# A new stored order of stretches and a new row of PSUM pairs in a hand-ordered Nystrom attention and expert FFN kernel

## The chip, the cores and the metric

The kernel runs on one core of a Trainium2 chip. The metric is device time in microseconds, the median over several runs of the same compiled program. Everything is one launch.

## The reference, cut to what matters

The input `x` has 16 batches of 1024 rows of 256 values, all float32. Each batch passes through a Nystrom attention and then through an FFN with a choice of one expert of eight.

```python
x = x + layernorm(attention(layernorm(x)))
x = x + layernorm(ffn(layernorm(x)))

# attention: 16 heads of 16 values, 64 landmarks
Q, K, V = split(x @ w_qkv); Q = Q / 4
Q_l, K_l = means of Q and K over groups of 16 rows
kernel1 = softmax(Q @ K_l.T); kernel2 = softmax(Q_l @ K_l.T); kernel3 = softmax(Q_l @ K.T)
SV = (kernel1 @ inverse(kernel2)) @ (kernel3 @ V)     # inverse by 6 iterations of 64x64 products
out = SV @ w_proj

# ffn
recon_e = relu(x @ Wd1[e] + bd1[e]) @ Wd2[e] + bd2[e]     # for all 8 experts
idx = the expert with the least mean of (recon_e - x)**2, for each batch
out = x @ W_base + b_base + relu(x @ Wa_down[idx] + ba_down[idx]) @ Wa_up[idx] + ba_up[idx]
```

## The kernel before, in words

Every batch passes through five pieces of work, each written as a Python generator that yields at the start of each **stretch**, a handful of instructions that belong together.

- `stage_a(b)` makes Q, K and V of batch b and the part `kernel3 @ V`. Its stretches: `stats` and `xn` (normalisation, on DVE), `qk` (matmuls `pq`, L475), `v` (`pv`, L500), `max` (`psm`, L547, with a DVE reduction `mx`, L556), `mcol` and `mrow` (row maxima), `e3` (scores `psc`, L567 and L578, and ACT's exponential, L588), `ut` (`put`, L604, with a DVE addition, L614) and `u` (a transpose `pu`, L653).
- `stage_p(b)` makes the inverse of kernel2. Its stretches are a serial chain: `k2`, `k2n`, `sums`, `kv0`, then six times `l` (matmuls `pxl`, then ACT's copy `qw`, L780), `h` (DVE, L783) and `q` (matmuls `pxq`, then DVE's L787 and L762), and `end`.
- `stage_c(b)` makes kernel1, the product and the projection. Its stretches: `max` (`psc`, L823, with the DVE reduction `most`, L831, and then POOL's `maxima`, L340 to L344), `mt` (a transpose `pm`, L853), `e1` (`psct`, L862 and L870, with ACT's exponential, L880), `sv` (`psv`, L891), `po` (`po`, L926, with ACT's copies and squares, L420 and L423, and POOL's `rstd`, L371) and `out` (DVE, L411).
- `stage_d1(b)` makes the experts' losses. Its stretches: `stats`, `xn`, `xt` (transposes `pt_d`, L404), `ht` (`ph`, L999), `df` (`pr`, L1029, with DVE's subtraction, L1037, and ACT's two squares, L1040), `pe` (a DVE reduction, L1057), `gather` (a matmul `pl`, L1062, and DVE's choice of the expert, then two DMA loads from SP) and `wup`.
- `stage_d2(b)` makes the FFN's output. Its stretches: `a` (`pad`, L1125, with ACT's `a_t`, L1134), `po` (`pf`, L1145 to L1158) and `out` (DVE, L411, and the store from SP).

Five streams run through these stages: stage a over all batches, stage p, stage c, the FFN of all batches but number 14, and the FFN of batch 14 alone. A stored string, `ORDER`, has one digit for each stretch: the stream that takes the next step. No planner runs when the kernel is built. The loop that emits the instructions does only this:

```python
    with tc.manual_schedule(engines={mybir.EngineType.PE, mybir.EngineType.Activation, mybir.EngineType.DVE, mybir.EngineType.Pool}):
        for k in order:
            next(emitted[k], None)
```

So the instructions of PE, ACT, DVE and POOL stand, on each engine, in the order of the digits, and each engine works through its own list in that order. Semaphores hold an instruction back until its data or its buffer is there. An order can therefore not make the result wrong, but it decides who waits.

The second string, `PAIRS`, decides buffers. All matmul results go to PSUM, whose eight banks are used as four pairs. Each request for a result tile takes the pair that the next digit names, and its first matmul waits until whoever held that pair before has been read out:

```python
    pairs = iter(PAIRS)

    def two_banks(shape, name, dtype=F32):
        return ps2 if isinstance(ps2, Nothing) else ps2.tile(shape, dtype, tag=f"ps2_{next(pairs)}", name=name)
```

Three buffers in SBUF matter below. The tile of `kt` is used again for the normalised rows `xn` of the next batch, so `xn` waits for the last `e3` of this batch. `x1` has two buffers, so `max` of stage c for batch b follows the FFN's end of batch b-2. And the last batch lends some buffers of earlier stages. In `turned_rows` and `stage_d2` the last batch also runs 20 and 16 matmuls without use (`spare`, L157) ahead of its transposes and of `pad`.

## Time and profile before

| what | value |
|---|---|
| median of 3 runs | 1941.46 us (1941.35 to 1944.79) |
| profiled execution, its own time | 1940.27 us |
| its span, first to last instruction | 1938.1 us |
| instructions in the span | 81528 |
| PE busy | 1844.0 us, 95% of the span |
| weight loads (PEld) busy | 1265.7 us, 65% |
| DVE busy | 1511.4 us, 78% |
| ACT busy | 1133.1 us, 58% |
| POOL busy | 212.1 us, 11% |
| granted TensorE clock, mean | 0.990 |

The profiled execution took 2.2 us more than its span, and 1.2 us less than the median. In the views, a line gives a start and a duration in us, the engine, the source line, the operation, the tiles as out<-in, the shape and a count; the bracket at the end is the idle time of the engine just ahead, and who ended it. "issue" there means that nothing that the profile shows was being waited for.

### The profile page before, as it was taken

To read this page: it belongs to the slowest core of one execution; us is meant where nothing else is said; L and a number is where in the kernel's file an instruction comes from. 1 tells how busy PE (TensorE), PEld (TensorE's weight loads), DVE (VectorE), ACT (ScalarE), POOL (GpSimd) and SP (SyncE) were. 2 spreads that over 40 slices of the span, in tenths; PEclk is the share of its full clock that TensorE was granted. 3 is DMA by queue.
4 is the path that set the end of the run, shared out by engine and by line. 5 is a ranking of instruction groups with operands and counts; after the bars stand their busy time and mean duration, and the time that the engine had idled before them with its cause. 6 is when DMAs were issued, how large, how long until landed. Compare 5 with 4: busy or idle time off the path is not lost.

```text
span 1938.1 us, 81528 instructions
## 1 busy us (share of the span) xinstructions
PE 1844.0 (95%) x37175; PEld 1265.7 (65%) x37175; DVE 1511.4 (78%) x2805; ACT 1133.1 (58%) x2434; POOL 212.1 (11%) x423
## 2 busy tenths in 40 slices
PE   6789999999999999999999999999999999989898
PEld 5667578567585766677676666866758485755544
DVE  6787878878788787787788887888788877686664
ACT  1243745573847557665655756557474667456576
POOL 1001001001110101101010010101101010010101
PEclk9899999999999999999999999999999999999899
DMA  8011011102020110111110111110201110010101
GB/s 203 3 25 25 3 28 47 24 18 56 7 67 3 51 24 12 40 29 46 28 34 15 29 45 28 46 24 8 67 7 46 24 51 2 7 46 7 45 6 48
DMA packets 65767, 64.30 MB, mean 33 GB/s; under 512 B 9244, under 2 KB 65424, under 8 KB 65424
## 3 DMA queue, kind: packets, MB, share of 16 engines
q1 hardware_dynamic: 65424, 59.11, 11.7%
q8 instruction: 291, 4.77, 1.0%
q14 instruction: 52, 0.43, 0.1%
HBM read 42.32 MB, written 16.78 MB: 30 GB/s over the span
## 4 chain that ended last, share of the span: by engine, by line
PE 78%; DVE 11%; ACT 5%; issue 2%; DMA 2%; POOL 1%; SPq 1%; DVEq 0%; POOLq 0%; ACTq 0%
PE ph L999 10%; PE pq L475 10%; PE pr L1029 10%; PE pf L1158 6%; PE pv L500 5%; PE po L926 5%; PE psv L891 4%; PE psct L862 3%; PE psc L823 3%; PE psm L547 3%; PE pxl L698 3%; PE psc L578 3%; PE pxq L698 3%; PE put L604 2%; DVE mx L556 2%
## 5 line engine op out<-in xcount | busy, mean ns | idle before, releaser
L1040 ACT ACTIVATE df<-df,bd_sb 128x512 f32<-128x512 f32 x512 | 362.7, 711 | 80.8 <-DVE df L1037 80.6
L1037 DVE TENSOR_TENSOR df<-pr,xt_d 128x1024 f32<-128x1024 f32 x256 | 298.7, 1215 | 58.2 <-PE pr L1029 45.6
L475 PE MATMUL pq<-xa,wqkv_sb 32*128 32x256 f32 x4096 | 242.5, 382 | 15.6 <-DVE xa L390 15.4
L1029 PE MATMUL pr<-ht,wd_sb 64*64 64x512 f32 x2048 | 245.6, 599 | 1.0 <-ACT ht L1007 0.2
L999 PE MATMUL ph<-xt_d,wd_sb 128*128 128x512 f32 x512 | 236.5, 604 | 2.1 <-issue 0.9
L475 PEld LDWEIGHTS pq<-xa,wqkv_sb 32*128 32x128 f32 x4096 | 219.4, 187 | 28.9 <-DVE xa L390 15.4
L556 DVE TENSOR_REDUCE mx<-psm 128x2 f32<-128x1024 f32 x128 | 149.8, 1217 | 37.4 <-PE psm L547 36.9
L999 PEld LDWEIGHTS ph<-xt_d,wd_sb 128*128 128x128 f32 x512 | 92.0, 189 | 116.2 <-issue 94.4
L831 DVE TENSOR_REDUCE most<-psc 128x16 f32<-128x1024 f32 x128 | 150.2, 1216 | 14.1 <-PE psc L823 13.9
L880 ACT ACTIVATE e<-psct 128x1024 f32<-128x1024 f32 x128 | 123.8, 1019 | 60.9 <-PE psct L870 60.6
L1029 PEld LDWEIGHTS pr<-ht,wd_sb 64*64 64x64 f32 x2048 | 67.6, 132 | 120.5 <-issue 56.4
L588 ACT ACTIVATE e<-psc 128x1024 f32<-128x1024 f32 x128 | 122.9, 1025 | 31.4 <-PE psc L578 30.9
L926 PE MATMUL po<-wproj_sb,svn 32*128 32x256 f32 x2048 | 126.9, 380 | 1.5 <-DVE svn L962 1.4
L1007 ACT ACTIVATE ht<-ph,bd_sb 128x1024 f32<-128x1024 f32 x64 | 70.9, 1108 | 93.7 <-PE ph L999 93.5
L500 PE MATMUL pv<-wqkv_sb,xa 32*128 32x256 f32 x2048 | 124.7, 379 | 0.1
L926 PEld LDWEIGHTS po<-wproj_sb,svn 32*128 32x128 f32 x2048 | 108.7, 185 | 19.4 <-DVE df L1037 4.9
L1158 PE MATMUL pf<-wbase_sb,xt_d 128*128 128x256 f32 x512 | 120.0, 388 | 0.0
L500 PEld LDWEIGHTS pv<-wqkv_sb,xa 32*128 32x128 f32 x2048 | 109.3, 185 | 6.9 <-issue 1.0
L1158 PEld LDWEIGHTS pf<-wbase_sb,xt_d 128*128 128x128 f32 x512 | 95.3, 191 | 22.7 <-issue 10.9
L783 DVE SCALAR_TENSOR_TENSOR q<-qw,eye 128x512 f32<-128x512 f32 x96 | 65.2, 679 | 45.1 <-ACT qw L780 44.7
L787 DVE SCALAR_TENSOR_TENSOR xw<-xw,pxq 128x640 f32<-128x640 f32 x96 | 69.7, 726 | 39.2 <-PE pxq L698 38.4
L1040 ACT ACTIVATION_READ_ACCUMULATOR df<-df,bd_sb 128x1 f32 x512 | 96.7, 189 | 0.0
(185 smaller groups left out, 3054.7 us busy)
## 6 DMA issues: line engine op xcount, KB each, us to landing
x<-in_L_attn_x_dram SPq DMA_DIRECT2D x16, 1024.0 KB
xa<-in_L_attn_x_dram SPq DMA_DIRECT2D x60, 256.0 KB
out_dram<-y_d SPq DMA_DIRECT2D x30, 512.0 KB
wqkv_sb<-in_L_attn_w_qkv_dram SPq DMA_DIRECT2D x12, 256.0 KB
wup<-in_L_ffn_Wa_up_dram SPq DMA_DIRECT2D x30, 64.0 KB
xa<-in_L_attn_x_dram SPq DMA_DIRECT2D x8, 128.0 KB
wproj_sb<-in_L_attn_w_proj_dram SPq DMA_DIRECT2D x4, 256.0 KB
out_dram<-y_d SPq DMA_DIRECT2D x4, 256.0 KB
```

Source lines behind the costliest of these rows:

```text
L475: nc.tensor.matmul(pq[g // 2][:, g % 2, 0 : N // 4], lhsT=wqkv_sb[rows32(g), k, f0 : f0 + P], rhs=turned[rows32(g), k], start=(k == 0), st ...
L500: nc.tensor.matmul(pv[g // 2][:, g % 2, 0:D], lhsT=turned[rows32(g), k, t0 // 4, :], rhs=wqkv_sb[rows32(g), k, 2 * D : 3 * D], start=(k == 0),
L556: nc.vector.tensor_reduce(mx3[:, n, q : q + 2], psc[g], X, ALU.max)
L588: nc.scalar.activation(e, psc[g], AF.Exp)
L831: nc.vector.tensor_reduce(mx[:, t0 : t0 + 2, 2 * g : 2 * g + 2].rearrange("x t p j -> x p t j"), psc[g].rearrange("x p t c (r l) -> x p t ...
L880: nc.scalar.activation(e, psc[g], AF.Exp)
L926: nc.tensor.matmul(po[g // 2][:, g % 2, 0:D], lhsT=svt[rows32(g), k, :], rhs=wproj_sb[rows32(g), k, :], start=(k == 0), stop=(k == ND - 1),)
L999: nc.tensor.matmul(ph[:, n, :], lhsT=wd1_sb[:, k, 2 * i : 2 * i + 2, :].rearrange("p e h -> p (e h)"), rhs=xt[:, k, n * 512 : (n + 1) * 51 ...
L1029: nc.tensor.matmul(pr[to, r, :], lhsT=wd2_sb[half, i, k * P + 64 * f : k * P + 64 * f + 64], rhs=ht[half, cols], start=True, stop=True,)
L1037: nc.vector.tensor_tensor(df, pr, middle(xt[:, k, cols], 2), ALU.subtract)
L1040: nc.scalar.activation(df[:, r, :], df[:, r, :], AF.Square, bias=bd2_sb[:, e, k : k + 1], accum_out=part[:, e, k * NW + n : k * NW + n + 1],)
L1158: nc.tensor.matmul(banks[j // 2][:, j % 2, :], lhsT=xt[:, k, cols], rhs=wbase_sb[:, k, :], start=False, stop=(j % 2 == 1 and k == NC - 1),)
```

## The change

Both stored strings are replaced: `ORDER` (1648 digits, the same number of each digit) and `PAIRS` (1634 digits). Nothing else in the file differs. Each engine gets the same instructions with the same shapes, in another sequence; result tiles land in other PSUM pairs; and the number of stand-alone semaphore instructions, which are put in where an instruction has more than one wait, goes from 335 to 325 on PE, from 416 to 403 on DVE and from 302 to 286 on ACT.

```diff
 ORDER = (
-    "0000020000012000000000000011000000012110130011010010110121010110120101201100000122120122020000202012"
-    "0112120112312013021310332001312132013303102333301301000133100030113003000330101102121023130112012213"
+    "0000020000010100000000001000000000111210130010100112012012101011001021100010010122120122020000202012"
+    "2131021011212003103301033001301333010100033313320120102001203333310001011102311013221021331102001221"
...
-    "3231333131231133331323331321133133122313122311312113121133212331224424422442224224422244444224244442"
-    "344423333334333443333343343333333433443333244333"
+    "2012212232113133313313312213331321233121232131131233133213312222244441421242244224224422424444224244442434"
...
 PAIRS = (
-    "0123012301230123012301230123012301203120312032103120312031203120310321032013201320123102310321032103"
+    "0123012301230123012301230123013201230123012301230123012301230123012031023103210321302123012013201320"
...
```

Written out as stretches (stream letter, batch, name), four places that the prediction speaks of. A stretch that only touches DVE or ACT is listed where it is emitted.

The start, after `p.0.k2`:

```
before: c.0.max.0.0 a.0.v.1 a.0.max.0.0 a.0.max.1.0 a.0.max.0.1 a.0.max.1.1 a.0.mcol a.0.mrow a.0.e3.0 ... a.0.u p.0.kv0 c.0.max.0.2 p.0.l0 p.0.h0 a.1.qk.0.0 p.0.q0
after:  a.0.v.1 p.0.k2n a.0.max.0.0 a.0.max.1.0 a.0.max.0.1 a.0.max.1.1 a.0.mcol a.0.mrow a.0.e3.0 ... a.0.u p.0.kv0 p.0.l0 p.0.h0 c.0.max.0.0 p.0.q0 a.1.qk.0.0
```

The choice of the expert of batch 13:

```
before: d.13.df.3.1.0 d.13.df.3.1.1 p.15.l2 c.14.e1.1.0 c.14.out.0 d.13.pe p.15.h2 d.13.gather p.15.q2
after:  d.13.df.3.1.0 p.15.h2 d.13.df.3.1.1 c.14.po.0 p.15.q2 c.14.e1.1.0 d.13.pe d.13.gather p.15.l3
```

The start of stage c of batch 15:

```
before: p.15.q4 c.14.po.1 p.15.l5 p.15.h5 d.13.po.1 d.13.out.0 c.14.out.1 p.15.q5 c.14.end d.13.out.1 d.13.end p.15.end c.15.max.0.0 c.15.max.0.2 d.14.stats.0 d.14.stats.1 c.15.mt.0
after:  p.15.q4 c.14.sv.1.1 d.13.po.1 d.13.out.0 c.14.po.1 p.15.l5 d.13.out.1 d.13.end p.15.h5 c.14.out.1 c.14.end c.15.max.0.0 c.15.max.0.2 c.15.mt.0 d.14.stats.0 d.14.stats.1
```

The last projection and the turn of batch 15's rows:

```
before: c.15.po.1 d.15.stats.0 d.14.df.3.0.0 d.14.df.3.0.1 d.14.df.3.1.0 c.15.out.1 d.15.stats.1 d.15.xn.0 d.15.xn.1 d.15.xt.0
after:  c.15.po.1 d.14.ht.3 d.15.stats.0 d.14.df.2.1.0 c.15.out.1 d.14.df.2.1.1 d.15.stats.1 d.15.xn.0 d.15.xn.1 d.15.xt.0
```

More of the change, by code (lines that the diff above doesn't have):

```diff
@@ L21 @@
 ORDER = (
-    "0000020000012000000000000011000000012110130011010010110121010110120101201100000122120122020000202012"
-    "0112120112312013021310332001312132013303102333301301000133100030113003000330101102121023130112012213"
-    "3201313001213030003201201000002133200020003312203013013023020111001022113212210302232033030100333133"
-    "0133133310333333210313001012213311221030211331112100103322303030230200002312013003102223312301000133"
-    "3313103333223133333130231300122133112213211030203001033221303030202033130010221022302331223133330321"
@@ L27 @@
-    "0333313010003333332103013001022131311221031021312330013322030302020012311100102303003022233113010001"
-    "3331330210013313323233313330213123002122330001301233233322030301332331233132121331133231333331331223"
-    "3331302003200210123021312010301200100020133200020003312203013033032331233132121333313321333311113333"
-    "3202300122033211202133222101023010120100001010100101330001022303330302011203133112311120331231122133"
-    "3322321333100110202130301230220113312013332031300000131312303030012013330303303311123123313212313332"
@@ L32 @@
-    "3112231333223213333101300131033110230132011003201200100020133200020001011223033303010200203023112030"
-    "0302223312310100333132231010001333002210013322233321333211001330221030313113311130330200203232323300"
-    "3122133223201201333331012013133313123331321233120332010313000010213001330012013330303303311110200112"
-    "0012003102331300100033332232033323232333333211033101023032022302331001133230122033030113321323133123"
-    "3113313213331313321212333331301120013011232132112321220102031020010033200330013023323302031211212223"
@@ L37 @@
-    "3231333131231133331323331321133122313122311312113121133212331224424422442224224422244444224244444442"
-    "344423333334333443333343343333333433443333244333"
+    "0000020000010100000000001000000000111210130010100112012012101011001021100010010122120122020000202012"
+    "2131021011212003103301033001301333010100033313320120102001203333310001011102311013221021331102001221"
+    "3321313001123030003201201000002133200020003312203013013020201110032121132121203022320120133301010003"
+    "3313322133331223020033313330010020303012230011313113311130330200203223323220302232033313333030333311"
@@ new lines @@
+    "3010003333332103103001022131310212302133001012333122020112013012103311100103112011300302223312301000"
+    "1333313103333223133333312033001022101332230211312330013322030130302020111001023113012101230220332301"
+    "0001333313033133231233333130233100122133223211030312030013322030130302020111001023112231021201230221"
+    "3330103333131100033331310333333201313001022101332230211311123100103322303030302002002223212231010232"
+    "1021033310100033313301223333131133331033200331120123311201110313230020333020110200213321323202132000"
@@ new lines @@
+    "2320133210201320133332123020333313103333332103103110010331012301111330020333030201102000330220330030"
+    "2223323010001333313103333223133333130233100122133110212300211312330013322030302302103121120011120022"
+    "0302232013330101000333120011001120212312301033331233331333002133012201331311131313033030200120302213"
+    "2223103022312331030103333131103333130103333332103103001022101332230211311123100103322303030302002002"
+    "2232120302232013330101000333330331333133333312033001022101332230211312330013322030330203312132121331"
@@ L39 @@
+    "1123133331131333321022123233313211330013321023030031220112030102313331002030023133213311113323133300"
+    "2012212232113133313313312213331321233121232131131233213312222244421441242224224422424444224244442434"
+    "243333334334443343334333333444333333433332444333"
 )
 PAIRS = (
-    "0123012301230123012301230123012301203120312032103120312031203120310321032013201320123102310321032103"
-    "2013201323012301230123012301230123012301203120312013201320132013203120310231021032103210321032103231"
@@ L43 @@
-    "0231023102310231032103210321023102310231203120312031203120312031023102310231023012301203102310321023"
-    "1023102310231203120132031203120312031203013203120310231021302103210321032103210321032103201320310231"
-    "0231023102310213021320132013201320132013201312023103210320132013201320132013201320132013201302103210"
-    "3210321032103210321032103210231023012301232031320132031203102301230123012301230123012310231023103210"
-    "3210321032103201320123012301302130213021302102310213102310321032013201320132013210321032103210321032"
@@ L48 @@
-    "1032103120312031203120310231021032103212031203210321032103210321032103120312031230123012301230123012"
-    "3102312031203120312031203123012301230123013201320132012301230123102310231023102310321032103210312031"
-    "0231023102310231023102310231203120313201320132013120310231023120312031203120310231023103210321032103"
-    "2103201320132013210321032103210321032103120312031203213021032103210321032103210321032103210321032103"
-    "2130213012301230123012302132013203120123012301230123012132013201320132012301320132013203120312031203"
@@ L53 @@
-    "1203120132013201302130213021302130213012130213021302130213021030213032103201320132012301230120312031"
-    "2031203120132013201320132103210231023102310231023102310232102310321032130213021302130213021302130213"
-    "0123012301230132013201321032103210321032103210312301230123013210321032103120312031203120230123010231"
-    "2031203120312031203120312031203102310231302103210321032103210321032013201320312031203120312031203102"
-    "3102310231021302132012301230123021"
+    "0123012301230123012301230123013201230123012301230123012301230123012031023103210321302123012013201320"
@@ new lines @@
+    "1230123012031201320132013201320132013201320132031201320130213201302130213021302130213021302130213021"
+    "3021320132013201302130213021320132013201320132013201320132013201230123012301230213021301230132012301"
+    "2301230123012301203120321031203210321032103210320312031203120312031203102310231023102310231203102310"
+    "2310231023102310231023103210320132013210231203120132013201320123012301320132013201320132013201321023"
+    "1023102310231023012301320132013201320132013202131023102310231023102310231023102310231203120321032102"
@@ new lines @@
+    "3120312031203120310231021302130210231023102310203121032013201320132013201320132013201321032103120312"
+    "0321032103210321031203102310231023102310231023102321303210321032103210231023102310231023102310231203"
+    "1230123013201320132013203123012302130123021302130213023102023102321032102310231023103210321032103210"
+    "3201321032103210321031203120310213021302130213021302130213021320312013201321032103210321032103210321"
+    "0312013201320132013201321032102310231023102310231023130212301320132013201320132013201320132013201320"
@@ new lines @@
+    "1320132013201230123012301320123012310231021301230120312031203120312032013201230123013201320132013201"
+    "3201321032103210321032103210320310231023102310231023102310230132031203120312031230123012301230123012"
+    "3012301320130213012301230123021301230120312031231023102310203132013201320132013201320132013012301230"
+    "1230123012301230123012301230123012301203102310123012301230123012032102310231023102310232130123012301"
+    "2301201320132103213021302312031023102321013201320132013201320132103201320132103210321032103210321032"
@@ L58 @@
+    "1032103210320132013201320132013210"
 )
```

## The prediction

> **What bounds the kernel now.** I read the page first, then a table of busy time by stretch of the run, then the timeline of PE where it stands idle, then the instruction order of both programs. These lines of the page say who is busy and what ended last:

> ```profile
> PE 1844.0 (95%) x37175; PEld 1265.7 (65%) x37175; DVE 1511.4 (78%) x2805; ACT 1133.1 (58%) x2434; POOL 212.1 (11%) x423
> ...
> q8 instruction: 291, 4.77, 1.0%
> ...
> PE 78%; DVE 11%; ACT 5%; issue 2%; DMA 2%; POOL 1%; SPq 1%; DVEq 0%; POOLq 0%; ACTq 0%
> ```

> PE is busy for 1844.0 of 1938.1 us. A new order takes no matmul away, so all that it can move is PE's idle 94.1 us. The windows view shows where that lies (columns: window, its length, then PE, PEld, DVE, ACT and POOL busy, granted clock, DMA):

> ```profile
> 0.00:200.00 200.00, 163.75 (x3765) 131.79 (x3765) 148.70 (x288) 64.76 (x109) 23.20 (x53) 0.97 0.28 62
> 200.00:1700.00 1500.00, 1469.82 (x30246) 1013.38 (x30242) 1208.76 (x2231) 920.10 (x1976) 162.81 (x317) 1.00 0.11 30
> 1700.00:1800.00 100.00, 90.25 (x1902) 58.35 (x1896) 69.65 (x128) 62.92 (x142) 10.44 (x21) 0.98 0.10 29
> 1800.00:1938.10 138.10, 120.12 (x1272) 62.19 (x1272) 84.24 (x160) 85.37 (x208) 15.66 (x33) 0.95 0.10 31
> ```

> The fifteen hundred microseconds in the middle hold only 30 us of idle; 64 us lie in the first 200 and the last 238. Of those 64, 15.4 us are the wait for the first rows and 6.4 us follow the last matmul, and no order changes them.

> Idle time on PE is of two kinds here. The first is a wait for another engine. The largest one (timeline) stands at the start of stage c of batch 15:

> ```profile
> 1795.99 1.38 PE L823 MATMUL psc<-bd,qt 32*128 32x128 f32 x36
> ...
> 1801.67 4.61 DVE L831 TENSOR_REDUCE most<-psc 128x16 f32<-128x1024 f32 x4
> ...
> 1807.74 0.61 PE L853 MATMUL pm<-ident_b,maxima 128*128 128x128 bf16 x4 [9.00 <-POOL maxima L342]
> ```

> The second kind has no releaser. PE stops in the middle of a group of equal matmuls (timeline of PE):

> ```profile
> 1444.05 0.61 PE L578 MATMUL psc<-bd,kt 32*128 32x128 f32 x14
> 1446.14 0.82 PE L578 MATMUL psc<-bd,kt 32*128 32x128 f32 x18 [1.49 <-issue]
> ```

> There are 15 such stops over 0.2 us, 16.3 us in all. They are not scattered: counted in weight loads, matmuls and semaphore instructions of PE's list, each falls 192 or 193 instructions past a multiple of 256. The q8 line gives the cause: 291 packets of 4.77 MB are 16.4 KB each, 256 instructions of 64 bytes, and 291 times 256 is PE's whole list. In the DMA records the packet that belongs to a stop starts 0.5 to 2.0 us ahead of it, and PE goes on 2.3 to 2.8 us after that packet's start. So PE has run through one block of instructions before the next arrived. It happens where instructions are short: 128 `psv` matmuls with their loads (256 instructions) take 1.3 us, a block of `pq` takes 7.2 us.

> **The change part by part.** Instructions are the same, so each term is a change in PE's waiting.

> *Instruction blocks.* I gave each group of matmuls its usual time in the trace (start to next start: `pq`, `pv`, `po`, `ph`, `pf` 3.6 to 3.7 us, `pr` 0.9, `psv` 1.26, `put` 1.0, `pxl` and `pxq` 0.73, `psc` 0.56 to 0.60; together 1850 us against 1844.0 busy) and summed, for every block limit, the time of the 310 instructions ahead of it, the look-back that parts stops from none best. Before: below 3.0 us 6 limits, all stopped, 7.3 us; 3.0 to 4.0 us 23 limits, 3 stopped, 2.9 us; above 6 stopped, 6.2 us. The new order has 4 below 3.0 (4 x 1.21 = 4.8 us), 17 between (17 x 0.125 = 2.1), and I leave 6.2 for the rest: 13.1 us, so **-3.2 us**. Bounds: 4.8 us if only the sure ones stop (-11.5), 25 us if every limit below 4.0 us stops (+9).

> [...]

> *The choice of the expert of batch 13.* `pl` (L1062) waits for DVE's `pe`, which needs ACT's squares of the last `df`:

> ```profile
> 1764.29 1.46 PE L862 MATMUL psct<-qt,bd 32*128 32x512 f32 x8
> 1765.25 0.71 PE L870 MATMUL psct<-mt,minus_max 32*128 32x512 bf16 x4
> 1767.89 0.36 PE L1062 MATMUL pl<-pe,ones 128*128 128x8 f32 x2 [1.93 <-DVE pe L1057]
> ```

> Before, 2.4 us of PE work (one `pxl`, one `psct`) stand between the last `pr` and `pl`; after, `po`, `pxq` and `psct`, 6.1 us. The wait was 1.93 us and gets 3.7 us more cover: **-1.9 us**, or nothing if ACT's queue is as much longer, since `po` adds 3.5 us of copies and squares ahead.

> *Stage c of batch 15.* `mt` follows DVE's four reductions (4.6 us) and POOL's `maxima` (1.4 us), and those follow `c.14.out.1`. New chain from the end of `c.14.po.1` on PE: ACT 3.6, POOL 1.3, DVE 1.7, then 4.6 and 1.4: 12.6 us. PE's own work meanwhile is `pxl` and two `max`, 3.3 us, so it stands for 9.3 us instead of 9.0. Before, `d.13.po.1` (5.2 us) and `p.15.q5` (0.6) lay in that time and `mt` came 18.0 us after `c.14.po.1`; now the one is done earlier and the other follows. 18.0 - 5.2 - 0.6 = 12.2 against 12.6: **nothing** gained, -1 to +1.

> *The start.* `c.0.max.0.0` (1.5 us of PE, 2.4 of DVE) moves behind the inverse's first step, so batch 0's reductions start at about 41.6 instead of 43.14 us. But then nothing stands between `kv0` and `l0`, where DVE needs 1.5 us, and `c.0.max.0.2` is still to be done. By my chain the new order is 0.8 us behind at `q0`, and has more to put into the 4.7 us of idle at 92 to 122 us. I take **nothing**, -2 to +2.

> *The rest.* For each PE instruction that waits for another engine I compared the PE work since the matmul that it hangs on with the durations in between (0.06 us for each hand-over, an estimate). In the middle part 15 had too little cover, 133 under 0.5 us to spare, 247 under 1.0; they waited 0.05, 0.07 and 0.005 us on the mean. The new order has 20, 141 and 260: 5 x 0.05 + 8 x 0.07 + 13 x 0.005 = **+0.9 us**. From 1700 us on, 12 with too little become 9 at 0.20 us and 19 under 0.5 become 23 at 0.08: **-0.3 us**.

> Sum: -3.2 - 1.9 - 0.3 + 0.9 = -4.5 us. The profiled execution took 1940.27 us, its span and 2.2 around it, and would take 1935.8; on the median, 1.2 above it, 1941.5 - 4.5 = 1937.0 us.

> **Rivals.** *The end eats the gain.* After batch 15's transposes the new order leaves four `df` of batch 14 instead of one. Each costs ACT 1.41 us (two squares at 0.71), 4.2 us more, and two DVE subtractions (1.2 each) now stand in the chain from `c.15.po.1` to `xt.0`: 6.6 us, 1943.6. For it: ACT's records follow each other without a pause for long stretches from 1885 us on. Against it: ACT idles some 12 us between 1868 and 1917, PE only 1.1.

> *Neighbours that hang on each other* (slower). `pu` needs DVE's addition to `ut` right after the matmuls `put`. Before, only batch 0 has nothing between; it waited 3.10 us, because DVE had 5.2 us of `xn` first. The new order has too little cover at batches 4, 9, 10 and 15 too. At 3.1 us each that is 12.4 us, 1949.4. It decides where DVE still has over half a microsecond of other work when `put` ends. At batch 4 it has: 6.9 us from `e3`'s end against 5.8 of PE. Against it: in the middle part such places waited 0.05 us on the mean.

> *Blocks of instructions* stop PE at every limit below 4.0 us (slower): +9 instead of -3.2, 1949.2. Against it: 20 of 29 such limits passed before.

> **The numbers.** Forecast 42%, the end 27%, neighbours 20%, blocks 11%. About 0.2% (3.9 us) can be told from no change; the forecast lies just beyond, the end's case within, the other two above. The range reaches down to 1928, where only the sure stops are left (1937.0 - 8.3), and up to 1950 for the two slower cases.

> **What would show it.** Right: stops without a releaser of 10 to 16 us at the counted limits; `pl` of batch 13 without a wait; again 9 us ahead of `pm` of batch 15; PE idle in the middle part within 3 us of 30. Wrong: that gap under 6 us, waits of `pu` over 1 us in several batches, or 8 us more or less in the middle part.

## The result, and the profile after

The changed kernel took 1932.56 us (median of 5 runs, 1931.63 to 1935.23) beside 1942.55 us of the kernel before; the ratio is 0.9949, 95% interval 0.9934 to 0.9963. Run again beside other runs of the kernel before (under "The last stretches") it was 0.9962, 0.9948 to 0.9976. The forecast was 1937.0 us, 4.5 us less than before; the gain was 7 to 10 us. The profiled execution took 1931.63 us and its span was 1929.7 us, 8.4 less than before.

The page of the changed kernel, the lines that answer to those of before (busy time, the instruction queue, the chain):

```profile
PE 1836.1 (95%) x37175; PEld 1260.4 (65%) x37175; DVE 1511.2 (78%) x2805; ACT 1131.7 (59%) x2434; POOL 211.9 (11%) x423
...
q8 instruction: 291, 4.77, 1.0%
...
PE 74%; ACT 11%; DVE 11%; issue 2%; POOL 1%; DMA 0%; SPq 0%; DVEq 0%; POOLq 0%; ACTq 0%
```

PE's busy time fell by 7.9 us, with the same 37175 matmuls, and its idle time from 94.1 to 93.6. The prediction had put the whole gain into the idle time. By stretch of the run (window, length, then PE, PEld, DVE, ACT, POOL busy, granted clock, DMA):

```profile
0.00:200.00 200.00, 162.36 (x3649) 129.73 (x3650) 148.69 (x292) 65.75 (x114) 20.87 (x49) 0.95 0.28 62
200.00:1700.00 1500.00, 1469.46 (x30567) 1017.00 (x30565) 1217.00 (x2255) 923.35 (x1978) 167.35 (x325) 1.00 0.12 31
1700.00:1800.00 100.00, 87.77 (x1721) 54.17 (x1714) 73.37 (x130) 58.86 (x134) 11.70 (x25) 0.92 0.08 25
1800.00:1938.10 138.10, 116.45 (x1253) 59.52 (x1251) 72.18 (x131) 83.72 (x209) 11.99 (x24) 0.98 0.06 19
```

The middle has 30.5 us of idle, as before, but 321 matmuls more were done in it. Idle time alone misleads here, so I aligned the two traces by work: each matmul counts its usual time, and the moments are compared at which equal sums are reached. At 200 us of the run the new order is 0.7 us ahead, at 1657 us 6.3, at 1828 us 12.1, and at the end 8.4. So the middle part gained 5.6 us, the zone of batch 15's attention 5.8, and the last 110 us gave 3.7 back.

### The profile page after: what moved, and what is told of

It reads as the page before. It is cut to its first block, busy times and chain, and to the rows that moved or that the text cites. A ratio compares the mean times of both kernels' runs of the same rounds, so it can differ in the third digit from the quotient of the medians.

```text
span 1929.7 us, 81483 instructions
## 1 busy us (share of the span) xinstructions
PE 1836.1 (95%) x37175; PEld 1260.4 (65%) x37175; DVE 1511.2 (78%) x2805; ACT 1131.7 (59%) x2434; POOL 211.9 (11%) x423
## 3 DMA queue, kind: packets, MB, share of 16 engines
q8 instruction: 291, 4.77, 1.0%
## 4 chain that ended last, share of the span: by engine, by line
PE 74%; ACT 11%; DVE 11%; issue 2%; POOL 1%; DMA 0%; SPq 0%; DVEq 0%; POOLq 0%; ACTq 0%
PE pq L475 12%; PE ph L999 10%; PE pr L1029 7%; PE pv L500 6%; ACT df L1040 6%; PE pf L1158 5%; PE po L926 4%; PE psv L891 4%; PE psct L862 3%; PE psc L823 3%; PE psm L547 3%; PE pxl L698 3%; DVE mx L556 2%; PE psc L578 2%; PE pxq L698 2%
## 5 line engine op out<-in xcount | busy, mean ns | idle before, releaser
L1037 DVE TENSOR_TENSOR df<-pr,xt_d 128x1024 f32<-128x1024 f32 x256 | 297.0, 1215 | 52.3 <-PE pr L1029 39.0
L1029 PE MATMUL pr<-ht,wd_sb 64*64 64x512 f32 x2048 | 240.8, 597 | 1.7 <-ACT ht L1007 1.2
L880 ACT ACTIVATE e<-psct 128x1024 f32<-128x1024 f32 x128 | 124.0, 1022 | 66.4 <-PE psct L870 66.2
L831 DVE TENSOR_REDUCE most<-psc 128x16 f32<-128x1024 f32 x128 | 150.2, 1216 | 13.5 <-PE psc L823 10.3
L500 PE MATMUL pv<-wqkv_sb,xa 32*128 32x256 f32 x2048 | 125.6, 379 | 0.1
L891 PEld LDWEIGHTS psv<-w_bd,e 128*32 128x32 f32 x8192 | 77.3, 109 | 34.2 <-issue 11.9
L483 ACT ACTIVATE qt<-pq 128x512 f32<-128x512 f32 x64 | 34.7, 595 | 107.7 <-PE pq L475 107.7
```

The costliest lines, as they stand in the source:

```text
L500: nc.tensor.matmul(pv[g // 2][:, g % 2, 0:D], lhsT=turned[rows32(g), k, t0 // 4, :], rhs=wqkv_sb[rows32(g), k, 2 * D : 3 * D], start=(k == 0),
L831: nc.vector.tensor_reduce(mx[:, t0 : t0 + 2, 2 * g : 2 * g + 2].rearrange("x t p j -> x p t j"), psc[g].rearrange("x p t c (r l) -> x p t ...
L880: nc.scalar.activation(e, psc[g], AF.Exp)
L891: nc.tensor.matmul(psv[rows32(g), j // 2, col : col + 2 * (HD + 1)], lhsT=es[p // 2][:, p % 2, g * P + 32 * j : g * P + 32 * j + 32], rhs= ...
L1029: nc.tensor.matmul(pr[to, r, :], lhsT=wd2_sb[half, i, k * P + 64 * f : k * P + 64 * f + 64], rhs=ht[half, cols], start=True, stop=True,)
L1037: nc.vector.tensor_tensor(df, pr, middle(xt[:, k, cols], 2), ALU.subtract)
```

## The experiments

Three measures return below. *Stops* are PE's idle times of over 0.1 us without a releaser, summed over the trace. *Clock* is PE's busy time in stretches at half clock (granted 0.5 in the records of both profiled executions), times one half: an estimate of what it lost. Matmuls in the stretches of before and of the changed kernel took 1.6 to 1.9 times their usual steps. *Rest* is the span less both.

### Where the blocks of instructions end

Short matmuls of constants ahead of everything lengthen PE's list without moving the work. They lie in the 15 us in which PE waits for the first rows. `PAIRS` gets one digit more at its head, for their tile.

```diff
+        shift = two_banks([P, 512], "shift")
+        for _ in range(64):      # 128 in the control
+            nc.tensor.matmul(shift[:, 0:4], lhsT=ones_b, rhs=ones_b[:, 0:4], start=True, stop=True)
         for k in order:
             next(emitted[k], None)
```

*After, 128 instructions more:* 

> The changed kernel with 64 short matmuls of constants ahead of everything, in the 15 us in which PE waits for the first rows. They add 128 instructions to PE's list, so every limit of a 256-instruction block falls half a block earlier in the work; nothing else is moved. Theory (PE stops where it runs through a block before the next has arrived): with the look-back of 310 instructions, limits below 2.5 us of work go from 1 to 13, 2.5 to 3.0 us from 3 to 9, 3.0 to 4.0 us from 17 to 28; at 1.2, 0.9 and 0.2 us each that is 9.4 to 30.7 us of stops, so about 1954 us (+21), between 1946 and 1962, and stops at other places, again at one residue of the instruction count. Rival (the stops belong to the work and not to the count, for instance to a port or to the weight loads): the stops stay at the same work and the time within 2 us of 1932.6.

*After, 256 more:* 

> The control: 128 such matmuls, 256 instructions, one whole block. The limits fall where they fell. Theory: within 2 us of the changed kernel, 1930.5 to 1934.5, with the stops at the same matmuls as there. Rival (the extra matmuls themselves, or a warmer clock at the start, move the time): the same difference as with 128 instructions, half or double of it.

*Before, 128 more:* 

> The kernel before with 64 short matmuls ahead of everything (128 instructions). Theory of blocks: limits below 2.5 us go from 3 to 18, 2.5 to 3.0 us from 3 to 11, 3.0 to 4.0 us from 23 to 28: 13.2 to 38.4 us of stops, so 1942.5 + 25 = 1967.7 us, between 1957 and 1977. Then the new order would be about as much ahead with shifted limits as without, some 13 us. Rival (stops belong to the work): within 2 us of 1942.5.

Measured: 1981.59 us (ratio to before 1.0206, 1.0183 to 1.0228), 1931.61 (0.9959, 0.9943 to 0.9975) and 1982.21 (1.0228, 1.0201 to 1.0254). Half a block cost 50 us in the changed kernel, a whole block nothing: with 256 more, 12 of the changed kernel's 13 stops come back at the same matmuls. So the stops belong to the count of instructions and not to the work; the rival falls. The size was missed: 50 us for the 21 expected, and 42 for 25; and the 13 us of lead that were expected with shifted limits are not there. The list of waits of the changed kernel with 128 more (waiter, waited for: sum, times, longest):

```profile
PE psv L891 <- issue: 20.2, 17, 2.3
...
PE pxl L698 <- issue: 5.5, 5, 1.7
PE put L604 <- issue: 4.2, 5, 2.1
```

Where the unaltered changed kernel has five stops in front of `psv`, 5.3 us, this one has seventeen. All stops together go from 10.2 to 43.0 us, and every one still falls at the same place of the count, within three instructions. Before with 128 more has 50.9 instead of 16.3. Stops are 33 us of the 50. A further part is what comes behind a stop (timeline of PE, then windows with the granted clock as the third number from the end, both of the changed kernel with 128 more):

```profile
316.85 0.92 PE L604 MATMUL put<-e,v_ones 128*32 128x64 f32 x49
319.86 0.42 PE L604 MATMUL put<-e,v_ones 128*32 128x64 f32 x13 [2.08 <-issue]
```

```profile
317.30:320.70 3.40, 1.31 (x62) 1.04 (x54) 2.44 (x5) 1.62 (x8) 1.20 (x2) 1.00 0.00 0
320.70:324.10 3.40, 3.40 (x56) 3.03 (x52) 1.94 (x6) 1.94 (x2) 0.00 (x0) 0.51 0.02 5
```

In the 3.4 us that hold the stop of 2.08 us, PE is busy for 1.31; in the next 3.4 us PE is busy throughout at a clock of 0.51, 1.7 us lost by the measure above. The changed kernel loses 12.5 us to this, with 128 more 25.6.

These two account for nearly the whole. Compared matmul by matmul with the unshifted changed kernel, from start to start, the steps that end at a limit of either list are 39.0 us longer and those in half-clock stretches 11.7, and the span is 50.5 us longer. In before it is 42.8 and 4.2 of 43.6. So some of a stop is hidden in the modelled ends of PE's matmuls: idle time shows 33 of the 39 us.

The two orders, 10 us apart as stored, are level with their limits shifted: 1981.59 and 1982.21. The lead does not outlast the shift, but the two are level for two reasons that cancel: the changed kernel still has 7.9 us fewer stops (43.0 for 50.9) and loses 6.6 us more to the clock (25.6 for 19.0). Both stored orders sit at a favourable place; by the work in the 310 instructions ahead of each limit, a shift by half a block gives five times as many limits below 3.0 us in either order (29 for 6, and 22 for 4).

### The kernel before, moved to its own best shift

The same edit, 116 matmuls, in the kernel before.

> The kernel before with 116 short matmuls of constants ahead of everything, 232 instructions, so the limits of blocks fall 24 instructions later in the work than now. By the look-back (mean stop for each range of work, from the six traces of the first runs) limits under 2.9 us of work go from 6 to 2 and the stops from 16.1 to 13.3 us. Theory (the lead of the new order is in good part where its limits fall): 2.8 us of stops and the clock that falls behind the longest of them, 1936 to 1938.5 against 1940 to 1942.5. Rival (the lead lies in the order and the pairs themselves): within 1.5 us of before.

Measured: 1938.67 us, ratio 1.0003 (0.9992 to 1.0015). The rival's number came. The stops did fall, from 16.3 to 13.6 us (13.3 expected), but the clock lost 16.1 us instead of 13.3, and the one paid for the other. It did so over all runs: the granted clock was 0.9888 on the mean of twelve runs and 0.9897 on that of 29 runs of before beside them, 1.8 us of the span. Why the clock fell is not shown. So the look-back forecast the stops here, and fewer stops were not a shorter time; that the changed kernel's lead comes from where its limits fall is not shown by this run.

### The last stretches

```diff
-ORDER = changed
+ORDER = changed[:1596] + before[1596:]     # PAIRS likewise, renamed at the joint
```

> The changed kernel's order and pairs up to the last projection of batch 15, and the order and pairs of before from there (52 stretches, pairs renamed so that the four holders agree at the joint). Aligned by work, the changed kernel gains 12.1 us up to there and gives 3.7 back after it. If the tail's order is the cause (four df of batch 14 left behind the last transposes instead of one): 1932.6 - 3.7 = 1928.9 us, between 1927.5 and 1930.5. Rival (the loss at the end belongs to what came before, for instance to work put off): no gain, 1931.5 to 1933.5, or a loss.

Measured: 1931.53 us, 0.9955 (0.9943 to 0.9968), beside 0.9959 of the control on the same chip: no gain in the time, so the rival's number. The trace, of the slowest of the six runs, shows two things that cancel: ahead of the joint, where all instructions are the changed kernel's, this execution had lost 4.6 us (one more stretch at half clock and two longer ones, and 7.25 us instead of 6.74 ahead of `pm`), and behind the joint it was 3.4 us faster. Over all runs the granted clock was 0.9887 on the mean and 0.9898 in the control's five, some 2 us more lost here.

The same with a joint at 1510 stretches, some 200 us from the end:

> The changed order for the first 1510 of 1648 stretches, the order of before for the last 138 (from 1720 us on), pairs renamed at the joint. Aligned by work, the changed kernel is 11 us ahead at the joint and ends 8.4 ahead. Theory (the gain lies in the middle part: stops at block limits and the clock that follows them; the last 200 us lose): the 1.9 us wait before pl returns and the tail's loss of 3.7 goes: 1932.6 - 2.6 = 1930.0 us, between 1928.5 and 1932.0. Rival (the gain is made in the last 200 us, where the forecast saw its -1.9 and -0.3): 1935 us or more.

Measured: 1927.35 us (1926.13 to 1928.34), 0.9940 (0.9924 to 0.9956). The theory's side. The last 110 us of work take 121.9, 122.2, 122.0 and 121.8 us in four profiled executions with the tail of before (before itself, the joint at 1596, this one, and before with 116 matmuls), and 125.6, 125.4, 125.4 and 125.2 in four with the new tail (the changed kernel twice, and the two with another start and with `po` ahead, below). The new tail costs 3.5 us. Its waits of over half a microsecond behind the last transposes (timeline of PE, changed kernel) have no counterpart in before:

```profile
1872.65 1.95 PE L1029 MATMUL pr<-ht,wd_sb 64*64 64x512 f32 x16 [0.73 <-ACT ht L1007]
...
1899.75 0.39 PE L1145 MATMUL pf<-bias_rows,chosen 24*128 24x512 bf16 x2 [0.62 <-DVE df L1037]
1905.86 0.36 PE L1062 MATMUL pl<-pe,ones 128*128 128x8 f32 x2 [1.01 <-DVE pe L1057]
```

The last two of these places in before, without a wait:

```profile
1909.02 0.39 PE L1145 MATMUL pf<-bias_rows,chosen 24*128 24x512 bf16 x2
...
1913.96 0.28 PE L1062 MATMUL pl<-pe,ones 128*128 128x8 f32 x2
```

That version with 124 matmuls ahead of it, and the changed kernel again, on one chip:

> The version that did best so far (changed order for 1510 stretches, tail of before) with 124 short matmuls ahead of everything, 248 instructions, so that limits fall 8 instructions later; by the look-back 12.3 us of stops instead of 13.5. Theory: 1 us less at most, 1925.5 to 1928.5, and below the changed kernel on the same chip by 3 to 6 us. Rival (its lead over the changed kernel was chance): within 1.5 us of the changed kernel beside it.

> The changed kernel itself, unaltered, beside the last run on one chip. Theory: 1931.5 to 1934, 3 to 6 us behind the version with the tail of before. Rival: within 1.5 us of it.

Measured: 1931.3 us, 0.9964 (0.9951 to 0.9976), and 1930.17, 0.9962 (0.9948 to 0.9976). Level: the version with the old tail did not show its lead here. Its trace has the shorter tail again, but 11.3 us of stops where 12.3 were expected and the unshifted one had 8.3, and 17.1 us lost to the clock against 13.6 of its neighbour and 10.3 unshifted; one half-clock stretch lies in the tail itself. That the old tail is 3.5 us shorter is shown in the traces; that the whole version is faster than the changed kernel is not confirmed.

### The choice of the expert of batch 13

> The changed kernel with one local step undone: c.14.po.0 and p.15.q2 go back behind the choice of the expert of batch 13, with their PSUM pairs. Between the last pr and pl stand 2.2 us of PE work again instead of 6.1. Theory (the wait before pl was hidden by these 3.9 us, of which 1.8 were to spare): a wait before pl of about 2.1 us and 1934.7 us, between 1933.5 and 1936. Rival (ACT's and DVE's queues were as much longer, or the gap opens again further on): no wait over 0.5 us there, or a time within 1 us of the changed kernel's 1932.6.

The kernel did something else than its text: within one stream the stretches keep their sequence, so `po` could not pass behind `psct`. What moved behind the choice were `psct` and `pxq`, and `po` came to stand on the PSUM pairs of the last two `pr`. Measured: 1935.39 us, 0.9975 (0.9965 to 0.9985). `po` then waited 3.12 us for DVE's `df`, and `pl` had no wait. It tells what a pair costs that is given away too late, and nothing on the step.

```diff
-... d.13.df.3.1.0 p.15.h2 d.13.df.3.1.1 c.14.po.0 p.15.q2 c.14.e1.1.0 d.13.pe d.13.gather ...
+... c.14.po.0 d.13.df.3.1.0 p.15.h2 d.13.df.3.1.1 c.14.e1.1.0 d.13.pe d.13.gather p.15.q2 ...
```

> The changed kernel with c.14.po.0 moved ahead of the last three pr groups of batch 13, with its PSUM pairs, and p.15.q2 behind the choice of the expert, so that only psct (2.2 us) stands between the last pr and pl, as before. (The earlier run with this aim moved something else: po stayed ahead of pl, psct and pxq went behind it, and po came to stand on the pairs of the last two pr.) Theory (the forecast's step): about 2 us of wait before pl and 1.9 us more, 1934 to 1935.5. Rival (the step is worth less than its wait, as in the run with the tail of before, where the wait of 1.93 us was back and only 0.7 us was lost by 60 us later): a wait of about 2 us, but no more than 1 us in the time.

In the kernel that ran, `po` stands ahead of the last two `pr` groups, not of three. Measured: 1936.62 us, 0.9988 (0.9974 to 1.0001), some 5 us more than the changed kernel on the same chip (0.9962); its span is 6.5 longer, and aligned by work the whole of it arises between 1705 and 1769 us. But the wait ahead of `pl` is not the cause (timeline of PE):

```profile
1752.05 1.95 PE L1029 MATMUL pr<-ht,wd_sb 64*64 64x512 f32 x16
1756.29 1.14 PE L862 MATMUL psct<-qt,bd 32*128 32x512 f32 x8 [2.29 <-DVE df L1037]
1757.26 0.39 PE L870 MATMUL psct<-mt,minus_max 32*128 32x512 bf16 x4
1758.07 0.60 PE L1062 MATMUL pl<-pe,ones 128*128 128x8 f32 x2 [0.42 <-DVE pe L1057]
1759.67 1.34 PE L698 MATMUL pxq<-qw,q 64*64 64x80 f32 x32 [1.00 <-ACT e L880]
```

`psct` waits 2.29 us for the pair that the last `pr` held, until DVE's `df` has read it, and `pl` only 0.42; a little later `pxl` waits 1.67 us, and the half-clock stretch here lasts 10.2 us instead of 3.4, which loses 1.8 us more. Both theories had the wait in the wrong place; moving stretches with their pairs moved the wait to the pair. So the step was not isolated by either run. The better witness is the version with the changed front and the old tail, which has the old sequence and the old pairs at this place: its `pl` waits 1.93 us again:

```profile
1755.09 0.36 PE L1062 MATMUL pl<-pe,ones 128*128 128x8 f32 x2 [1.93 <-DVE pe L1057]
```

Between 150 and 110 us of work from the end it takes 57.8 us, before 57.6, the changed kernel 57.0 and 56.8 in its two executions. In that stretch lies stage c of batch 15 too, so both steps together were worth 0.6 to 1.0 us of time. The clock blurs this: its half-clock stretches there lost 3.4 us in that version, 4.7 in before and 5.2 in both executions of the changed kernel. Without them the steps were worth 1.1 to 2.8 us, and whether the new order or chance brought the clock's part is not shown.

### The start

```diff
-ORDER = changed
+ORDER = before[:189] + changed[189:]
```

> The order of before for the first 189 stretches (to about 200 us), the changed order for the rest. Aligned by work, the changed kernel loses 1.3 us by 150 us and is 0.7 ahead at 200. Theory: the start is worth nothing, as forecast; limits of blocks move by 3 instructions (the count of stops by the look-back goes from 14.2 to 12.6 us): 1931 to 1934 us. Rival (the new start pays, since the chain of the first inverse is fed earlier): 1935 us or more; or it costs: 1930 or less.

Measured: 1932.21 us, 0.9968 (0.9956 to 0.9979). The interval overlaps both results of the changed kernel; the profiled spans are 1928.9 and 1929.7 us. The new start is worth nothing that can be told in the time, as forecast. The granted clock was 0.9909 on the mean of the twelve runs and 0.9895 of eight runs of the changed kernel, some 2.7 us less lost, so the two starts need not be equal in their waits.

### The PSUM pairs

```diff
-PAIRS = changed
+PAIRS = ("0123" * 409)[:1634]
```

> The changed order with the row of PSUM pairs replaced by a plain turn, 0 1 2 3 0 1 2 3 and so on, so that each result tile waits for the one four requests ahead. Theory (in the middle part, cover and not the pair decides): by my comparison of cover with durations, 38 matmul groups have too little cover instead of 44, the count of stops by the look-back is 13.4 us instead of 14.2: within 2 us of 1932.6. Rival (the searched row matters: a turn makes PE wait for the psct and pr tiles that ACT and DVE hold longest): 1938 us or more, with waits on ACT's L880 and DVE's L1037.

Measured: 1953.49 us, 1.0071 (1.0052 to 1.0090), slower than before, and 21 us longer in its span than the changed kernel. The theory falls. The rival's number came, but not its two waits, on L880 and L1037. Stops (10.1 us) and clock (13.3) are as in the changed kernel; compared matmul by matmul, 20.4 of the 21.0 us stand where PE waits for another engine, in small pieces, most of them between 300 and 1500 us. The list of waits and one of them in the timeline, PE and ACT:

```profile
PE put L604 <- ACT ut L612: 4.5, 5, 1.0
...
PE put L604 <- ACT qw L780: 3.0, 2, 1.5
...
PE psc L567 <- ACT ut L612: 2.3, 2, 1.9
```

```profile
872.02 1.10 PE L604 MATMUL put<-e,v_ones 128*32 128x64 f32 x64
...
876.82 0.39 PE L567 MATMUL psc<-mrow,ones_b 32*128 32x512 bf16 x2 [1.90 <-ACT ut L612]
```

```profile
873.43 1.04 ACT L420 COPY y_c<-po 128x512 f32<-128x512 f32 x2
...
876.42 0.35 ACT L612 COPY ut<-put 128x256 f32<-128x256 f32 x1
```

`put` is done at 873.1, but the copy that frees its pair takes 0.35 us and stands in ACT's list behind eight squares of `df`, two copies and four squares of `po`: it starts at 876.42. `psc` was given that pair and waits. My count of cover followed semaphores and durations along each chain, without what else stands in the queue of the engine in between; it said 38 tight places instead of 44.

## Why the prediction was right in its time and not in its terms

The sums of the profiled executions show what varies (us; the shifts lie ahead of everything):

| kernel | span | stops | clock | rest |
|---|---|---|---|---|
| before | 1938.1 | 16.3 | 13.3 | 1908.5 |
| changed | 1929.7 | 10.2 | 12.5 | 1907.0 |
| changed, again | 1928.1 | 8.9 | 13.6 | 1905.6 |
| changed, 128 more | 1980.2 | 43.0 | 25.6 | 1911.6 |
| before, 128 more | 1981.7 | 50.9 | 19.0 | 1911.8 |
| before, 232 more | 1937.7 | 13.6 | 16.1 | 1908.0 |
| changed front, old tail | 1925.5 | 8.3 | 10.3 | 1906.9 |
| changed, pairs in turn | 1950.7 | 10.1 | 13.3 | 1927.3 |

Spans from 1925 to 1982 us leave a rest within 7 us of each other, except where the pairs were taken away; in the six executions not in the table it lies between 1903 and 1910.3. Of the 8.4 us between before and changed, 6.1 are stops, 0.8 clock and 1.5 rest; in the second execution of the changed kernel it is 7.4, -0.3 and 2.9 of 10.0. The rest varies by as much as the difference that is split, so the split is sure for the stops alone.

*Instruction blocks: right in mechanism, the largest term, half its size.* Forecast -3.2 us to 13.1; it became -6.1, to 10.2. The mis-sized part is the four limits below 3.0 us that I called sure at 1.21 us each: one stopped, 1.2 us instead of 4.8. Why the others let PE pass is not shown: by a like look-back 52 of 55 such limits stopped PE in the two runs with 128 more. The limits between 3.0 and 4.0 us gave 2.2 us (forecast 2.1), the rest 6.9 (6.2). In the changed kernel 128 instructions without any work for the result cost 50 us. The prediction's times of the packets (0.5 to 2.0 us ahead of a stop, 2.3 to 2.8 to its end) hold for 14 of the 15 stops; for the shortest, at 1333 us, they are 2.7 and 3.0.

*What the sum left out: the clock behind a stop.* Two pauses of before, a stop at 640 us and a wait of 1.78 us for DVE's `q` at 1111, each cost 1.7 us more, by the measure above, in a half-clock stretch; the changed kernel's profiled execution had none between 121 and 1759 us, and one more than before near the start. In the middle part that is 3.4 us of the 5.6 gained, and partly luck: in its second profiled execution the same stop at 349 us did bring a half-clock stretch (below). Over all runs on one chip the clock has no part in the lead: it was 0.9895 on the mean of eight runs of the changed kernel and 0.9897 of 29 of before.

*"All that it can move is PE's idle 94.1 us": wrong.* Idle hardly moved, because waits for other engines grew by nearly what the stops lost. Busy time fell 7.9 us (6.5 in the second execution, with 3.6 of idle): a busy PE in this profile holds pauses. Compared with the median step between the same two neighbours, steps at full clock that are over 0.15 us too long sum to 35.8 us before and 28.7 after, with idle time taken out. Most have no releaser (28.8 and 19.5). The sums depend on what is taken as usual, that they fall does not; part of it stands at block limits, and what holds the others is not shown. No term of the sum foresaw it, so that the time came into the range is in good part luck.

*The choice of the expert: the wait went, most of the gain in time did not come.* The new PE list has `po` and `psct` there, and `pl` has no wait:

```profile
1755.61 0.59 PE L862 MATMUL psct<-qt,bd 32*128 32x512 f32 x2
1756.04 0.38 PE L870 MATMUL psct<-mt,minus_max 32*128 32x512 bf16 x2
1756.35 0.39 PE L1062 MATMUL pl<-pe,ones 128*128 128x8 f32 x2
1756.66 0.78 PE L698 MATMUL pxl<-xw,l 64*64 64x80 f32 x32
1758.24 0.34 PE L891 MATMUL psv<-w_bd,e 128*32 128x34 f32 x16 [0.79 <-ACT e L880]
1759.15 1.54 PE L891 MATMUL psv<-w_bd,e 128*32 128x34 f32 x112 [0.58 <-ACT e L880]
```

Forecast -1.9, found 0.6 to 1.0 us with the next step, or 1.1 to 2.8 with the clock's loss taken out: 0.79 and 0.58 us of it came back at once in `psv`, behind ACT's exponentials. That `po`'s copies and squares had pushed these back, as the bound "nothing" had supposed, is likely and was not tested alone.

*Stage c of batch 15: right.* 6.74 us ahead of `pm`, and 1.74 just before it, 8.5 together for 9.0:

```profile
1783.40 1.38 PE L823 MATMUL psc<-bd,qt 32*128 32x128 f32 x36
1786.52 1.69 PE L823 MATMUL psc<-bd,qt 32*128 32x128 f32 x28 [1.74 <-ACT qw L780]
1794.95 0.61 PE L853 MATMUL pm<-ident_b,maxima 128*128 128x128 bf16 x4 [6.74 <-POOL maxima L342]
```

*The rest by cover: wrong as a method.* Waits for other engines in the middle part grew by 4.1 us (2.2 in the second execution), not 0.9; the experiment with the pairs shows that such a count does not see queues. The count's 0.06 us for each hand-over is about what the trace of before has: medians of 0.054 us from ACT's end to PE's start and 0.056 from DVE's, in waits of over 0.15 us. Between 1657 and 1828 us of before they fell by 2.7, of which the two steps above are 2.4. But the forecast's -0.3 was for everything from 1700 us on, and in the last 110 us they grew by 2.5: with the two steps taken out, these waits came to some 2.6 us more, not 0.3 less. *The start:* 0.7 us at 200 us, within its -2 to +2.

*The rivals.* The end did eat 3.5 us, at half its price of 6.6 and by the first half of its mechanism: the `df` left behind the transposes made PE wait, while the chain to `xt.0` did not get longer (the wait ahead of the transposes is 1.28 us, before 1.55). The forecast's time held because the blocks gave twice as much and busy time fell unforeseen. Neighbours did hang on each other, at a sixth of the price each: `pu` before and after, the longest in both being batch 0's,

```profile
PE pu L653 <- DVE ut L614: 3.9, 3, 3.1
```

```profile
PE pu L653 <- DVE ut L614: 7.3, 9, 3.1
```

so the eight others wait 0.5 us on the mean, not 3.1, and together 3.4 us more than before. Blocks at every limit did not come: of the 21 limits below 4.0 us 6 stopped PE.

## What to carry to other kernels

When a long list of short instructions runs through one engine, count where its instruction blocks end before comparing two orders: a shift by half a block, 128 instructions, cost 50 and 42 us here, more than any reordering won, and a shift by a whole one is the control. Judge an order together with its buffer row, by the queue of the engine that frees the buffer and not by the duration of the freeing step: `psc` waited 1.90 us for a copy of 0.35, and the whole row in turn cost 21 us. And align two traces by work, since idle and busy time each mislead when pauses hide in modelled ends, as they did here: idle time showed 33 of 39 us.

## What the runs showed of the hardware

```profile
346.60:350.00 3.40, 2.29 (x89) 1.92 (x88) 3.20 (x4) 1.70 (x2) 0.00 (x0) 1.00 0.63 107
350.00:353.40 3.40, 2.11 (x116) 1.53 (x118) 1.17 (x4) 0.00 (x0) 0.00 (x0) 1.00 0.02 5
```

```profile
348.60:352.00 3.40, 1.48 (x139) 1.28 (x131) 1.94 (x2) 0.69 (x1) 0.00 (x0) 1.00 0.02 3
352.00:355.40 3.40, 3.40 (x50) 1.64 (x40) 1.71 (x4) 0.48 (x1) 0.00 (x0) 0.51 0.02 5
```

In the first the stop lies across two windows, with PE busy for 2.29 and 2.11 us of 3.40, in the second within one, with PE busy for 1.48. The clock's loss varied from 8.9 to 17.1 us between executions of nearly the same list (all but the two with 128 more), and that is as large as the difference that was to be predicted; 29 runs of the kernel before on one chip spread from 1932.4 to 1945.9 us.
